# A graph network in fp32: first group in two halves, statistics aggregated ahead, one more residual buffer, second weights' loads on another queue

## The chip, the core, the metric

One core of a Trainium2 chip runs the whole program. The metric is device time per execution in microseconds (us). Engines: PE is TensorE, DVE VectorE, ACT ScalarE, POOL GpSimd, SP SyncE.

## The reference, cut

`x` is 128 graphs of 128 nodes by 256 features, `adj` one 128 x 128 matrix for all. Four layers, each with a layer norm and relu ahead and a residual around it:

```python
h = relu(layernorm(x)); x = x + gated_messages(h, adj)     # layer 0
h = relu(layernorm(x)); x = x + causal_attention(h)        # layer 1
h = relu(layernorm(x)); x = x + three_graph_convs(h, adj)  # layer 2: 256 -> 512 -> 1024 -> 256
h = relu(layernorm(x))                                     # layer 3
y = (A_hat @ h) @ W1.T + b1                                # 256 -> 512
y = relu(batchnorm(y))       # statistics over all 128 x 128 rows
y = y @ W2.T + b2            # 512 -> 256
x = x + batchnorm(y)         # again over all rows
```

The two batch norms cut the work into three parts. The first pass takes 32 groups of four graphs through everything up to `z = (A_hat h) W1` and stores z and the residual x3 to DRAM. The second pass loads z again, normalizes it and multiplies by W2. The tail normalizes once more, loads x3 where it isn't loaded yet, adds and stores.

## The kernel before

Groups 0 to 31 are generators that a fixed string interleaves. For group 0 a string FILL does so at the start, with nothing beside it but group 1 and the preparation of the weights. Products are done by a seven-product scheme (`seven`) that needs sums of quarters first. The end of the first pass and the junction:

```python
# layer 3 of a group; zp has two buffers of z, and group 31's z takes those of group 30
z = ZT[g] = [zp.tile([P, 2, T], FP, tag="z", name=f"zo_{g}_{j}") for j in range(2)]
def put(ij, pb, other):
    ...
    nc.vector.tensor_tensor(dst, pb, other, ALU.add)          # L661
    ...
    if done.count(j) == 2:
        for jj in range(2):
            nc.vector.bn_stats(stats1[:, 2 * j + jj, g, :], z[j][:, jj, :])
        if g != LAST:
            nc.sync.dma_start(Z[g][:, 2 * j : 2 * j + 2, :], z[j])   # store of z, SP
... # cut
most1 = bn_part(stats1, FC, slice(LAST), "most1")   # four bn_aggr over 31 groups
... # rest of the last group
passA.close()                                       # the first pass's memory is free
... # cut
OWN, IN_PASS, IN_Z, ROOM = 5, 7, 13, 18             # residual buffers: 18
nc.scalar.dma_start(bw2T, BW2T)                     # second weights, on ACT's queue
nc.scalar.dma_start(bw2s, BW2S)
... # cut: load_z on SP; load_x3(g, queue=nc.gpsimd), one every fourth group
for n in range(1, 1 + AT_ONCE):
    load_z(n)
last1 = bn_part(stats1, FC, slice(LAST, NG), "last1")
sc1, sh1 = bn_affine(most1, last1, FC, g1_c, be1_c, "bn1", b1_c)   # the affine
```

Of the kernel before, what the change touches and what calls it, by code (L numbers as in the profile page):

```python
# [15 lines left out]
P = 128  # L16
# [6 lines left out]
def kernel(  # L23
# [41 lines left out]
    G = 4  # L65
# [23 lines left out]
    adj_sb = const.tile([P, P], FP, name="adj_sb")  # L89
    nc.sync.dma_start(adj_sb, adj)  # L90

# [4 lines left out]
    weights = passA.enter_context(tc.tile_pool(name="weights", bufs=1))  # L96
    xin = passA.enter_context(tc.tile_pool(name="xin", bufs=4))
# [6 lines left out]
    load_x(0)  # L104
# [20 lines left out]
    stats1 = zp.tile([P, FC, NG, 6], FP, name="stats1", bufs=1)  # L125
# [108 lines left out]
    SETS = {}  # L234

    def prepare():
# [21 lines left out]
        SETS["q"], SETS["v"] = seven_of(m_qk, "m_qk"), seven_of(w_vo, "w_vo")  # L258
        yield

        nc.vector.tensor_tensor(a2T, adjT, adjT, ALU.mult)
        SETS["1"] = seven_of(w1, "w1")
        yield
        SETS["2"] = seven_of(w2, "w2")
# [40 lines left out]
    def norm(g, layer):  # L305

        xt = X[g]
        st = small.tile([P, G, 6], FP, tag="st", name=f"st{layer}_{g}")
        mv = small.tile([P, G, 2], FP, tag="mv", name=f"mv{layer}_{g}")
        for b in range(G):  # L310
            nc.vector.bn_stats(st[:, b, :], xt[:, b, :])  # L311
        for b in range(G):
            nc.vector.bn_aggr(mv[:, b, :], st[:, b, :])
        rs = small.tile([P, G], FP, tag="rs", name=f"rs{layer}_{g}")
        nc.gpsimd.tensor_scalar(rs, mv[:, :, 1], LN_EPS, None, ALU.add)  # L315
        nc.gpsimd.tensor_tensor(rs, rs, nhalf[:, :G], ALU.pow)  # L316
        sh = small.tile([P, G], FP, tag="sh", name=f"sh{layer}_{g}")
        nc.gpsimd.tensor_scalar(sh, mv[:, :, 0], -1.0, None, ALU.mult)
        nc.gpsimd.tensor_tensor(sh, sh, rs, ALU.mult)  # L319
        h = w.tile([P, G, D], FP, tag="h", name=f"h{layer}_{g}", bufs=3)  # L320
        for b in range(G):
            nc.scalar.activation(  # L322
                h[:, b, :], xt[:, b, :], AF.Relu, bias=sh[:, b : b + 1], scale=rs[:, b : b + 1]
            )
        return h

    def mixed(dst, src, aT, name, evicts):

        for c in range(src.shape[-1] // P):
            pm = bank([P, G, P], f"{name}_{c}")  # L330
            for b in range(G):
                nc.tensor.matmul(  # L332
                    pm[:, b, :], src[:, b, c * P : (c + 1) * P], aT, start=True, stop=True
                )
            evicts[c % len(evicts)](dst[:, c, :], pm.rearrange("p b n -> p (b n)"))
# [84 lines left out]
    def layer0(g):  # L420

        xt = X[g]
        h = norm(g, 0)
        yield
        gl = small.tile([P, G, 3], FP, tag="gl", name=f"gl_{g}")
        gs = w.tile([P, D], FP, tag="gs", name=f"gs_{g}", bufs=1)
        for b in range(G):
            for i in range(3):
                nc.vector.scalar_tensor_tensor(  # L429
                    gs, h[:, b, :], 1.0, gw[:, i, :], ALU.mult, ALU.mult,  # L430
                    accum_out=gl[:, b, i : i + 1],
                )
            if b == 1:
                yield
        nc.vector.tensor_tensor(gl, gl, gb[:, None, :].to_broadcast([P, G, 3]), ALU.add)
        gt = small.tile([P, G, 3], FP, tag="gt", name=f"gt_{g}")
# [4 lines left out]
        um = w.tile([P, 2, G, D], FP, tag="um", name=f"m_{g}", bufs=1)  # L441
# [4 lines left out]
        for b in range(G):  # L446
            nc.scalar.activation(bias[:, b, :], eb, AF.Copy, scale=gt[:, b, 0:1])
            nc.scalar.activation(cmb[:, b, :], ain, AF.Copy, scale=gt[:, b, 0:1])
            nc.vector.scalar_tensor_tensor(
                cmb[:, b, :], aout, gt[:, b, 1:2], cmb[:, b, :], ALU.mult, ALU.add  # L450
            )
            nc.vector.scalar_tensor_tensor(
                cmb[:, b, :], ident, gt[:, b, 2:3], cmb[:, b, :], ALU.mult, ALU.add
            )
        yield
        for b in range(G):
            nc.vector.scalar_tensor_tensor(
                bias[:, b, :], oeb, gt[:, b, 1:2], bias[:, b, :], ALU.mult, ALU.add
            )
        pc = bank([P, G, P], f"pc_{g}")  # L460
        for b in range(G):
            nc.tensor.transpose(pc[:, b, :], cmb[:, b, :], ident)
        nc.vector.tensor_copy(cmbT, pc)
        yield
        for q in range(G // 2):
# [7 lines left out]
        nc.vector.scalar_tensor_tensor(xt, bias, 0.0, xt, ALU.max, ALU.add)  # L473
        yield

    def layer1(g):

        xt = X[g]
        h = norm(g, 1)
        yield  # L480
        hT = w.tile([P, DC, T], FP, tag="dT", name=f"hT_{g}", bufs=2)
        for c in range(DC):
            pt = bank([P, G, P], f"pt_{g}_{c}")
            for b in range(G):
                nc.tensor.transpose(pt[:, b, :], h[:, b, c * P : (c + 1) * P], ident)
            evict = nc.vector.tensor_copy if c else nc.scalar.copy
            evict(hT[:, c, :], pt.rearrange("p b n -> p (b n)"))
        ex = w.tile([P, 4, 1, T // 2], FP, tag="ex", name=f"hs_{g}", bufs=2)
        hs = sums(nc.vector, quarters_t(hT), ex, ex[:, 3])
# [3 lines left out]
        qv = w.tile([P, 2, DC, 2, D], FP, tag="qv", name=f"qv_{g}", bufs=1)  # L493
# [19 lines left out]
        yield from seven(product, put, [P, 2, D], f"pqv_{g}")  # L513
# [4 lines left out]
        ps = bank([P, G, P], f"ps_{g}")  # L518
        for b in range(G):
            for c in range(DC):  # L520
                nc.tensor.matmul(  # L521
                    ps[:, b, :], qv[:, b // 2, c, 0, (b % 2) * P : (b % 2 + 1) * P],
# [3 lines left out]
        p = w.tile([P, G, P], FP, tag="p", name=f"p_{g}", bufs=1)  # L526
        nc.vector.scalar_tensor_tensor(
            p, ps, 1.0 / D**0.5, maskb[:, None, :].to_broadcast([P, G, P]), ALU.mult, ALU.add
        )
        nmax = small.tile([P, G], FP, tag="nmax", name=f"nmax_{g}")  # L530
        nc.vector.tensor_reduce(nmax, p, AX.X, ALU.max, negate=True)
        psumr = small.tile([P, G], FP, tag="psumr", name=f"psumr_{g}")
        for b in range(G):
            nc.scalar.activation(
                p[:, b, :], p[:, b, :], AF.Exp, bias=nmax[:, b : b + 1],
                accum_out=psumr[:, b : b + 1],
            )
        rsum = small.tile([P, G], FP, tag="rsum", name=f"rsum_{g}")
        nc.vector.reciprocal(rsum, psumr)
        yield  # L540
        pp = bank([P, G, P], f"pp_{g}")
        for b in range(G):
            nc.tensor.transpose(pp[:, b, :], p[:, b, :], ident)
        pT = w.tile([P, G, P], FP, tag="pT", name=f"pT_{g}", bufs=1)
        nc.vector.tensor_copy(pT, pp)
        yield
        for q in range(G // 2):
            py = bank([P, 2, D], f"py_{g}_{q}")
            for r in range(2):
                b = 2 * q + r  # L550
                nc.tensor.matmul(py[:, r, :], pT[:, b, :], v_of(b), start=True, stop=True)  # L551
            for r in range(2):
                b = 2 * q + r
                nc.vector.scalar_tensor_tensor(
                    xt[:, b, :], py[:, r, :], rsum[:, b : b + 1], xt[:, b, :], ALU.mult, ALU.add
                )
        yield
        h = norm(g, 2)
        yield
        mT = w.tile([P, DC, T], FP, tag="dT", name=f"mT_{g}", bufs=2)  # L560
        mixed(mT, h, a2T, f"pm2_{g}", (nc.vector.tensor_copy, nc.scalar.copy))
        ex = w.tile([P, 3, 1, T // 2], FP, tag="ex", name=f"ms_{g}", bufs=2)
        ms = sums(nc.vector, quarters_t(mT), ex)
        yield
        u = w.tile([P, G, H1], FP, tag="um", name=f"u_{g}", bufs=1)

        def put(ij, pb, other):
# [8 lines left out]
        yield from seven(  # L576
            rows_by_half(ms, SETS["1"], H1 // 2), put, [P, 2, H1 // 2], f"pu_{g}"
        )
        uT = w.tile([P, HC1, T], FP, tag="uT", name=f"uT_{g}", bufs=1)
        mixed(uT, u, a2T, f"pmu_{g}", (nc.vector.tensor_copy,))  # L580
        ex = w.tile([P, 3, HC1 // 2, T // 2], FP, tag="us", name=f"us_{g}", bufs=1)
        US[g] = sums(nc.vector, quarters_t(uT), ex)
# [110 lines left out]
    FILL = "paaapaaaAaBBBBBABBBBBBBppABBAApBBABBBpBBAB"  # L693
    stream = {"a": layer0(0), "p": prepare(), "B": layer1(0), "A": part(layer0, 1)}
    for k in FILL:
        next(stream[k])
    assert all(next(stream[k], k) == k for k in "aAB")
    bs, ds = part(layer1, 1), stream["p"]
    next(bs)
    for g in range(NG):  # L700
        if g + AHEAD < NG:
            load_x(g + AHEAD)
        stream = {
# [7 lines left out]
    most1 = bn_part(stats1, FC, slice(LAST), "most1")  # L711
    for _ in ds:
        pass
    passA.close()

    def bn_affine(most, last, nch, gam, bet, name, bias):
# [3 lines left out]
        share = 1.0 / NG  # L720
# [24 lines left out]
    OWN, IN_PASS, IN_Z, ROOM = 5, 7, 13, 18  # L745
# [10 lines left out]
    nc.scalar.dma_start(bw2T, BW2T)  # L756
    bw2s = second_w.tile([P, 3, FC // 2, D // 2], FP, name="bw2s_late")
    nc.scalar.dma_start(bw2s, BW2S)
# [65 lines left out]
    last1 = bn_part(stats1, FC, slice(LAST, NG), "last1")  # L824
    sc1, sh1 = bn_affine(most1, last1, FC, g1_c, be1_c, "bn1", b1_c)
# [30 lines left out]
    sc2, sh2 = bn_affine(most2, last2, DC, g2_c, be2_c, "bn2", b2_c)  # L856
# [58 lines left out]
```

## Time and profile before

The median of four runs is 2615.83 us (2615.49 to 2616.07). PE bounds the kernel; this is the page's first part, busy time, share and count of each engine:

```profile
PE 2531.7 (97%) x15215; PEld 2280.8 (87%) x15215; DVE 1918.0 (73%) x4819; ACT 1283.9 (49%) x2575; POOL 292.1 (11%) x577
```

So only the places where PE waits can give time. I follow five markers through all traces: PE's first p_x (the start is over), the product pr of groups 0, 29 and 30, PE's first po_x (second pass), PE's last po (the start of its last line in the timeline), ACT's first o (tail). Between them lie the stretches of this table. The kernel before was traced four times (the trace of the prediction and three more, told below):

| stretch | before, 4 traces | mean |
|---|---|---|
| to the first p_x | 83.61, 85.97, 83.96, 85.09 | 84.66 |
| p_x to pr of group 0 (the first turn) | 57.67 to 57.68 | 57.68 |
| pr of group 0 to 29 | 2052.9 to 2053.0 | 2052.9 |
| pr of group 29 to 30 (the turn of group 30) | 68.67 to 68.68 | 68.68 |
| pr of group 30 to first po_x (the junction) | 71.40, 71.55, 71.71, 71.39 | 71.51 |
| first po_x to last po | 203.21, 203.48, 202.79, 203.22 | 203.18 |
| last po to first o | 5.35 to 5.36 | 5.36 |
| first o to the end | 67.84, 68.43, 68.27, 68.24 | 68.20 |

From the timeline of the kernel before (start us, us, engine, line, operation; in brackets the idle time before it and what ended it; SPq and POOL DMA lines are issues, not the transfers):

```profile
2314.64 0.62 POOL L778 DMA_DIRECT2D x3i<-x  x1 [0.34 <-issue]
...
2317.39 2.13 SPq L667 DMA_DIRECT2D z<-zo  x2
...
2321.71 1.27 SPq L766 DMA_DIRECT2D zi<-z  x3
...
2323.68 0.63 DVE L661 TENSOR_TENSOR zo<-pz_z,pz_t 128x512 f32<-128x512 f32 x1
...
2326.40 1.06 POOL L778 DMA_DIRECT2D x3i<-x  x2 [11.13 <-PE pz_x L377]
```

One x3 load goes out 2.8 us ahead of the two stores of z, and none beside them until the put of pz_z at 2323.68 is over. That put (the addition that writes a part of z) has no bracket: it waits for nothing. DVE is busy with an aggregation right up to it, though (2322.79, 0.98 us), so this trace doesn't show how long before it the store of group 30's z had landed.

### The profile page before, as it was taken

To read this page: it belongs to the slowest core of one execution; us is meant where nothing else is said; L and a number is where in the kernel's file an instruction comes from. In a line of the timeline stand start us, us, engine, line, operation; in brackets the idle time before it and what ended it. 1 tells how busy PE (TensorE), PEld (TensorE's weight loads), DVE (VectorE), ACT (ScalarE), POOL (GpSimd) and SP (SyncE) were. 2 spreads that over 40 slices of the span, in tenths; PEclk is the share of its full clock that TensorE was granted. 3 is DMA by queue.
4 is the path that set the end of the run, shared out by engine and by line. 5 is a ranking of instruction groups with operands and counts; after the bars stand their busy time and mean duration, and the time that the engine had idled before them with its cause. 6 is when DMAs were issued, how large, how long until landed. Compare 5 with 4: busy or idle time off the path is not lost.

```text
span 2610.6 us, 40551 instructions
## 1 busy us (share of the span) xinstructions
PE 2531.7 (97%) x15215; PEld 2280.8 (87%) x15215; DVE 1918.0 (73%) x4819; ACT 1283.9 (49%) x2575; POOL 292.1 (11%) x577
## 2 busy tenths in 40 slices
PE   4999999999999999999999999999999999989995
PEld 3999999999999999999999999999999999978875
DVE  7877777777777777777777777777777776567776
ACT  3544544444445454454444444554445444336656
POOL 1111111111111110111111111111011111010001
PEclk7999999999999999999999999999999999999998
DMA  3000000000000000000000000000000000034559
GB/s 132 15 33 33 33 23 27 33 33 33 26 26 31 33 33 33 33 33 17 33 33 33 33 25 25 33 33 33 33 33 29 21 25 25 25 143 163 176 174 398
DMA packets 49544, 143.06 MB, mean 55 GB/s; under 512 B 4146, under 2 KB 23108, under 8 KB 45380
## 3 DMA queue, kind: packets, MB, share of 16 engines
q1 hardware_dynamic: 40708, 111.37, 11.8%
q0 software_dynamic: 7632, 27.79, 2.9%
q8 instruction: 120, 1.97, 0.3%
q10 hardware_dynamic: 1008, 1.31, 0.1%
q14 instruction: 76, 0.62, 0.1%
HBM read 73.48 MB, written 66.98 MB: 54 GB/s over the span
## 4 chain that ended last, share of the span: by engine, by line
PE 91%; DMA 3%; DVE 2%; ACT 2%; issue 1%; POOL 0%; ACTq 0%; DVEq 0%; POOLq 0%; SPq 0%
PE p_x L377 17%; PE p_x L360 9%; PE p_z L377 8%; PE pmu L332 4%; PE p_z L360 4%; PE pu_x L360 4%; PE p_y L377 4%; PE pz_x L377 4%; PE pm L332 2%; PE pg L332 2%; PE ps L521 2%; PE py L551 2%; PE pqv_x L501 2%; PE p_y L360 2%; PE pm L469 2%; PE pqv_x L496 2%
## 5 line engine op out<-in xcount | busy, mean ns | idle before, releaser
L322 ACT ACTIVATE h<-x,sh,rs 128x256 f32<-128x256 f32 x512 | 268.8, 589 | 367.0 <-POOL sh L319 367.0
L377 PE MATMUL p_x<-uT,w 128*128 128x256 f32 x1024 | 242.2, 379 | 0.0
L608 ACT ACTIVATE h2T<-h2T 128x512 f32<-128x512 f32 x192 | 120.5, 628 | 227.3 <-DVE h2T L607 227.3
L377 PEld LDWEIGHTS p_x<-uT,w 128*128 128x128 f32 x1024 | 189.7, 190 | 23.1
L311 DVE BATCH_NORM_STATS2 st<-x 128x6 f32<-128x256 f32 x512 | 190.8, 415 | 4.9 <-DMA x<-in_x_dram 2.8
L315 POOL TENSOR_SCALAR rs<-mv 128x4 f32<-128x4 f32 x128 | 29.9, 233 | 1403.8 <-ACT h2T L608 1053.0
L429 DVE SCALAR_TENSOR_TENSOR gs<-h,gw 128x256 f32<-128x256 f32 x384 | 161.0, 419 | 28.4 <-ACT h L322 23.0
L392 ACT COPY p_t<-p_x 128x512 f32<-128x512 f32 (+1 forms) x192 | 96.6, 503 | 108.2 <-PE p_x L377 101.4
L316 POOL TENSOR_TENSOR rs<-rs,nhalf 128x4 f32<-128x4 f32 x128 | 148.9, 1163 | 0.0
L332 PEld LDWEIGHTS pmu<-a2T,u 128*128 128x128 f32 x1024 | 119.5, 192 | 15.1 <-issue 14.8
L360 PEld LDWEIGHTS p_x<-w,h2T 128*128 128x128 f32 x1024 | 124.3, 192 | 3.3
L574 ACT ACTIVATE u<-u 128x512 f32<-128x512 f32 x96 | 60.5, 631 | 134.8 <-DVE u L573 134.8
L789 ACT ACTIVATE zi<-zi,sh_bn,sc_bn 128x512 f32<-128x512 f32 x124 | 97.4, 812 | 55.9 <-DMA zi<-z 30.0
L360 PE MATMUL p_x<-w,h2T 128*128 128x128 f32 x1024 | 124.6, 275 | 0.0
L377 PE MATMUL p_x<-us,w_s 128*128 128x256 f32 x512 | 121.2, 379 | 0.0
L377 PE MATMUL p_x<-uT,w_s 128*128 128x256 f32 x512 | 121.1, 379 | 0.0
L377 PE MATMUL p_y<-uT,w 128*128 128x256 f32 x512 | 121.1, 379 | 0.0
L377 PE MATMUL p_z<-us,w 128*128 128x256 f32 x512 | 121.0, 379 | 0.0
L377 PE MATMUL p_z<-us,w_s 128*128 128x256 f32 x512 | 120.9, 379 | 0.0
L332 PE MATMUL pmu<-a2T,u 128*128 128x128 f32 x1024 | 119.8, 275 | 0.0
L637 DVE TENSOR_TENSOR x<-pr,x 128x512 f32<-128x512 f32 x64 | 43.7, 683 | 90.4 <-PE pr L636 90.4
L377 PEld LDWEIGHTS p_z<-us,w 128*128 128x128 f32 x512 | 97.3, 190 | 13.2
(289 smaller groups left out, 6174.7 us busy)
## 6 DMA issues: line engine op xcount, KB each, us to landing
z<-zo SPq DMA_DIRECT2D x62, 512.0 KB, 2.6
zi<-z SPq DMA_DIRECT2D x31, 1024.0 KB, 4.9
x<-in_x_dram SPq DMA_DIRECT2D x32, 512.0 KB, 4.0
x<-x POOLq DMA_DIRECT2D x32, 512.0 KB, 3.4
out_dram<-x3i SPq DMA_DIRECT2D x30, 512.0 KB, 13.5
x3i<-x POOLq DMA_DIRECT2D x21, 512.0 KB, 9.4
x3i<-x SPq DMA_DIRECT2D x11, 512.0 KB, 4.7
w<-in_L_gnn_W_dram SPq DMA_DIRECT2D x1, 2048.0 KB
```

Source lines behind the costliest of these rows:

```text
L311: nc.vector.bn_stats(st[:, b, :], xt[:, b, :])
L316: nc.gpsimd.tensor_tensor(rs, rs, nhalf[:, :G], ALU.pow)
L322: nc.scalar.activation(h[:, b, :], xt[:, b, :], AF.Relu, bias=sh[:, b : b + 1], scale=rs[:, b : b + 1])
L332: nc.tensor.matmul(pm[:, b, :], src[:, b, c * P : (c + 1) * P], aT, start=True, stop=True)
L360: nc.tensor.matmul(pb[:, rr, :], a_r[r][:, c, rr * P : (rr + 1) * P], b_r[r][:, c, :wide], start=(first and rr == 0 and c == 0), stop=(c = ...
L377: nc.tensor.matmul(pb[:, jj, :], b_r[r][:, c, at : at + P], a_r[r][:, c, :], start=(first and jj == 0 and c == 0), stop=(c == nk - 1), ski ...
L392: nc.scalar.copy(t, pb)
L429: nc.vector.scalar_tensor_tensor(gs, h[:, b, :], 1.0, gw[:, i, :], ALU.mult, ALU.mult, accum_out=gl[:, b, i : i + 1],)
L469: nc.tensor.matmul(pm[:, r, :], cmbT[:, b, :], h[:, b, :], start=True, stop=True)
L574: nc.scalar.activation(dst, dst, AF.Relu)
L608: nc.scalar.activation(dst, dst, AF.Relu)
L789: nc.scalar.activation(z, z, AF.Relu, bias=sh1[:, j : j + 1], scale=sc1[:, j : j + 1],)
```

## The change

Four parts, which I call H, A, R and W. **H**: group 0 goes through layers 0 and 1 and the first half of layer 2 as two halves of two graphs, so that one half's norm can run beside the other's products; the halves use plain products, as the sums of the seven-product scheme need the whole group. FILL is written anew for it, and a part of the preparation of the weights moves behind the halves. **A**: the four aggregations over 31 groups become four over 30, emitted a group earlier; two groups are left for the end. **R**: adj and stats1 move into the first pass's memory, and a 19th residual buffer fits. **W**: the second weights are loaded from SP's queue, not ACT's.

```diff
-    load_x(0)
+    X[0] = xin.tile([P, G, D], FP, tag="x", name="x_0")
+    for i in range(2):
+        half = slice(i * G // 2, (i + 1) * G // 2)
+        nc.sync.dma_start(X[0][:, half, :], x[half].rearrange("b n d -> n b d"))
... (norm, layer0, layer1 take a list of graphs bs; in layer1, for a half:)
-        yield from seven(
-            rows_by_half(ms, SETS["1"], H1 // 2), put, [P, 2, H1 // 2], f"pu_{g}"
-        )
+            for b in bs:
+                pb = bank([P, H1], f"pu_{g}_{b}")
+                for c in range(DC):
+                    nc.tensor.matmul(pb, mT[:, c, b * P : (b + 1) * P], w1[:, c, :], ...)
... (A)
+        if g == LAST:
+            most1 = bn_part(stats1, FC, slice(LAST - 1), "most1")
-    most1 = bn_part(stats1, FC, slice(LAST), "most1")
     for _ in ds:
         pass
+    last1 = bn_part(stats1, FC, slice(LAST - 1, NG), "last1")
     passA.close()
... (R; adj_sb moves likewise)
-    stats1 = zp.tile([P, FC, NG, 6], FP, name="stats1", bufs=1)
+    stats1 = weights.tile([P, FC, NG, 6], FP, name="stats1")
-    OWN, IN_PASS, IN_Z, ROOM = 5, 7, 13, 18
+    OWN, IN_PASS, IN_Z, ROOM = 6, 8, 14, 19
... (W)
-    nc.scalar.dma_start(bw2T, BW2T)
+    nc.sync.dma_start(bw2T, BW2T)
-    nc.scalar.dma_start(bw2s, BW2S)
+    nc.sync.dma_start(bw2s, BW2S)
```

## The prediction

> **What bounds the kernel now.** I read the 40 slices of the page first, then the table of windows over both ends, then the chain of work that ended last and the timeline of each engine there.
>
> ```profile
> PE   4999999999999999999999999999999999989995
> PEclk7999999999999999999999999999999999999998
> DMA  3000000000000000000000000000000000034559
> ```
>
> PE is full in 36 of 40 slices; in the waits of PE between 200 and 2250 us nothing is listed. Time can be had only in the first slice, around slices 36 and 37, and in the last three. The windows (busy us of PE, PEld, DVE, ACT, POOL, then granted clock, DMA share, GB/s) give the ends:
>
> ```profile
> 20.00:40.00 20.00, 7.21 (x21) 4.33 (x21) 15.63 (x49) 7.72 (x18) 5.92 (x9) 0.63 0.42 138
> 40.00:60.00 20.00, 15.26 (x70) 12.10 (x70) 15.06 (x38) 9.64 (x23) 0.00 (x0) 0.77 0.00 1
> 60.00:80.00 20.00, 14.79 (x78) 13.32 (x79) 14.88 (x41) 7.91 (x17) 2.81 (x4) 0.83 0.12 46
> 80.00:100.00 20.00, 20.00 (x121) 18.30 (x120) 17.89 (x60) 11.88 (x24) 3.31 (x8) 1.00 0.00 1
> ...
> 2320.00:2360.00 40.00, 30.67 (x127) 25.03 (x126) 30.86 (x67) 20.89 (x39) 4.23 (x7) 0.87 0.66 244
> ...
> 2580.00:2600.00 20.00, 8.04 (x54) 6.71 (x52) 9.22 (x15) 8.06 (x12) 0.58 (x2) 0.80 1.03 418
> ```
>
> Up to 80 us PE idles about 35 us and runs at a reduced clock; from 80 us it is full. At 2320 to 2360 it loses 9.3 us. In the tail the DMA engines are full at 418 GB/s. Pieces of the chain in the start (start us, us, what):
>
> ```profile
> 25.90 3.40 PE pm L469 x8
> ...
> 36.72 0.61 ACT h L322
> 37.37 1.96 PE pt L485 x7
> ...
> 52.22 0.50 ACT p L534 x2
> ...
> 64.56 0.61 ACT h L322
> 65.22 3.98 PE pm L332 x16
> ...
> 83.77 0.43 PE p_x L377 x2
> ```
>
> One group walks through two layers with nothing beside it: every norm is a walk DVE, POOL, ACT, PE. My marker for "the start is over" is the first p_x at L377, at 83.6 us in the timeline. The junction between the passes, from the timeline:
>
> ```profile
> 2324.82 0.99 DVE L675 BATCH_NORM_AGGREGATE mv_most<-stats 128x2 f32<-128x186 f32 x1
> 2324.96 1.13 PE L377 MATMUL pz_x<-gT,bw1T_s 128*128 128x256 f32 x4 [1.10 <-DVE zo L661]
> ...
> 2328.89 0.98 DVE L675 BATCH_NORM_AGGREGATE mv_most<-stats 128x2 f32<-128x186 f32 x1
> ...
> 2334.24 2.08 PE L800 MATMUL po_x<-zo,bw2T 128*128 128x256 f32 x4 [8.15 <-ACT zo L789]
> ```
>
> Four aggregations over 31 groups stand among the last statistics, and PE's second pass waits 8.15 us for what hangs on them.
>
> **What the Trainium skill says.** "TensorE: Matmul & The Clock Gate", Part 1 on the HAM clock gate: the array runs at half rate after about 3.4 us of idleness and needs about 3.4 us of work to come back. The trace agrees: pm x16 took 3.98 us at 65.22 and 1.79 us in the steady state. So pulling work closer saves twice, and an idle gap that only shrinks from 8 to 6 us still costs the slow phase. "SBUF — State Buffer", Who interferes with whom: a tensor_tensor with both inputs in SBUF contends with GpSimd's reads, under an exclusive lock. The trace agrees: the norm's four POOL steps took 0.24 + 0.23 + 1.04 + 0.28 = 1.8 us from 9.09 on, but 0.31 + 1.06 + 1.45 + 0.22 = 3.0 us from 33.52 on, when DVE did 128x1024 subtractions. "ScalarE: Activation LUTs", What ACT_TABLE_LOAD costs, has about 1283 ns; the trace shows 1.28 us for each. "DMA: Bandwidth & Descriptors", Where 436 GB/s comes from, puts the fabric at 435; the tail's 418 is near it, so there only bytes count.
>
> **The start, step by step.** I walked the new order of instructions on each engine with the durations above; all times here are my estimates from them. The first x comes in halves, but POOL does both halves' scalings before the first power, so h starts at about 11 us as before (11.29). The second weights (w1) are wanted on DVE at about 14 us, perhaps before they land; the gates of half one are ready at about 18 us, where the sigmoid's table load holds them, against 20.3. Its transposed mixing matrix is copied at about 22.5 to 23 (before 25.15), x is done at 27.5 (before 31.4), h of layer 1 at 33.6 (before 36.7), the first copies of hT at 35.3 (before 39.4). Half two comes some 4 us behind: its norm waits for DVE behind the copy of hT, its h ends at 39.9, its hT at 42.7.
>
> The plain product costs PE more. qv per group is 16 matmuls of 256 columns worth 0.43 us each (8 of them in pairs of 128 columns), 6.9 us for 7 x 0.86 = 6.0; u is 8 of 512 columns at 0.86, 6.9 for 6.0. That is 0.9 us each. It takes away the sums (8 x 0.42 us on DVE) and three rounds of kept copies and additions from the chain.
>
> Scores of half two stand before those of half one on PE. They come at about 47.5 (before, the whole group's at 50.5), exp at 49.2 to 50.3 (before 52.2 to 53.9). Then ACT takes sigmoid's table for group 1 and exp's table again, 2 x 1.28 us, before the exp of half one, which ends at about 54.8: here most of the lead is lost. From there: py at 56 to 57.2, x at 58.2, statistics at 59.5, POOL 1.7 us, h at about 61.7, where the kernel before had 65.2. PE's work from there to the marker at full clock: mixing and transposes 0.9, u 6.9, group 1's pm 1.7, pmu 3.6, transposes of bw1 and bw2 with small ones 2.1, sum 15.2; the slow clock adds some 2.2 (as 3.98 against 1.79) and the gap for copying mT 0.6. The marker is then at 61.7 + 18.0 = 79.7, **3.9 us earlier**.
>
> Some DVE work now lies behind the marker: eight subtractions for bw2t and bw1T at 0.34 us, ahT and vecs, 3.2 us together, in a window where DVE was busy 17.89 of 20. By my walk the hT copy that PE needs comes about 7.7 us after the marker and PE wants it at 9.5, so it is mostly hidden; I charge **0.5 us**.
>
> **The junction.** The 30 groups are aggregated in the last-but-one turn, where DVE has 19 to 26 us of work in 40; its pT copy and PE's py keep 1 us of slack there, the later norm about 3. So 4 x 0.98 us moves to where it is free. At the end, put of pz_z starts at 2323.05 rather than 2323.68, the last product at 2324.6 rather than 2324.96, its copy on ACT ends at 2326.35, the two last statistics at 2327.6, two aggregations at 2327.85; before, the affine's first step was at 2330.14. **2.3 us earlier**, as everything behind it (3.1 us of small steps, then ACT, then PE) is unchanged. The weights bw2T and bw2s were issued by ACT at 2326.14, after its last copy; now SP issues them behind the last stores of z, at about 2320. They carry 0.9 MB, 2.1 us at 418 GB/s, so the zi loads behind them on SP are later; the first zi is wanted at 2336.2 - 2.3 = 2333.9 and should be there by 2333.
>
> **The tail.** A 19th buffer takes one 0.52 MB load of x3 out of the full stretch (13 late loads for 14), into the second pass whose DMA share is 0.49: 0.52 MB / 418 GB/s = **1.25 us**. The room comes from adj and stats1 (3.5 KB per partition), which now go with the first pass.
>
> Sum: -3.9 + 0.5 - 2.3 - 1.25 = -6.95 us; 2616.0 - 7.0 = **2609.0 us**.
>
> **Rivals.** (a) The halves do not help: two walks on in-order queues hold each other up (POOL's powers, ACT's h behind h, the second exp table), and the marker stays near 83. For it: DVE was busy 15 of 20 us in each window, so it is nearly as much the bound as latency. Against it: the chain shows each engine waiting in turn. Time about 2613. (b) The halves overlap better than my walk: DVE's 57.5 us of work up to 80 with almost no idling after a first x at 6 us would put the marker near 70 to 72. For it: PE waits 8.1 and 6.2 us for h alone. Time about 2601. (c) At the junction the zi or bw2T load takes the place of the aggregation, since DMA runs at 410 to 426 GB/s from 2323 to 2337 and one more x3 load joins; the 2.3 us shrinks to 1 or less. Time about 2610.5. (d) The tail is hidden anyway, because ACT's 64 activations (45.3 us) pace it; against it, the DMA engines stay full for 20 us after ACT ends.
>
> **Range.** The start is the wide term: 0 to 10 us; junction 1 to 2.5; tail 1 to 1.5; backlog up to 2. Together 2603 to 2613.5. Two per cent is 52 us, more than all idle time that the change touches, so within 2% is nearly certain.
>
> **What would show it.** Right: first p_x near 79.7; full PE windows from there; L675's 31-group aggregations gone from the end and the affine's first step 2.3 us after less waiting; between last pz_x and first po_x some 6 us; 13 loads of x3 in the tail, its full stretch 1.25 us shorter. Wrong: PE idle in 80 to 130 us waiting for DVE; po_x waiting for a DMA; stalls of PE in the last-but-one turn; or the marker beyond 75 to 83.

## The result, and the profile after

The changed kernel takes 2612.15 us (median of four runs, 2611.57 to 2613.66) against 2615.83: a ratio of 0.9987, with a 95% interval from 0.997 to 1.0004, "same" at 2%. The number lies in the predicted range, 3.15 us above the point.

That says little about the reasons. The 40 slices of the page after:

```profile
PE   5999999999999999999999999999999999989996
PEclk8999999999999999999999999999999999989998
```

The first slice is a step fuller; the dip at slice 36 is as in the kernel before. The same windows as in the prediction (busy us of PE, PEld, DVE, ACT, POOL; clock, DMA share, GB/s):

```profile
20.00:40.00 20.00, 9.52 (x33) 6.44 (x33) 16.63 (x48) 4.04 (x12) 5.33 (x8) 0.66 0.39 130
40.00:60.00 20.00, 13.16 (x70) 10.05 (x69) 15.18 (x56) 13.20 (x29) 3.44 (x9) 0.90 0.00 1
60.00:80.00 20.00, 17.33 (x73) 12.07 (x72) 11.63 (x35) 5.58 (x14) 3.49 (x8) 0.76 0.00 0
80.00:100.00 20.00, 19.99 (x117) 17.77 (x117) 18.18 (x60) 13.79 (x29) 1.96 (x4) 1.00 0.12 47
2320.00:2360.00 40.00, 29.21 (x121) 23.33 (x119) 26.00 (x60) 20.24 (x37) 4.21 (x7) 0.83 0.71 254
```

In the start PE is busier (17.33 for 14.79 between 60 and 80 us, in part because its clock is lower there, 0.76 for 0.83), and from 80 us it is full. But between 2320 and 2360 PE lost 1.5 us instead of gaining two (29.21 for 30.67), although DVE has less to do there (26.00 for 30.86). The start, in PE's timeline:

```profile
63.77 1.22 PE L352 MATMUL pm<-a2T,h 128*128 128x128 f32 x4 [2.67 <-ACT h L338]
...
66.48 5.11 PE L635 MATMUL pu<-w,mT 128*128 128x512 f32 x8
...
73.16 3.60 PE L635 MATMUL pu<-w,mT 128*128 128x512 f32 x8
...
82.27 1.99 PE L397 MATMUL p_x<-uT,w 128*128 128x256 f32 x8
```

The last half's h reaches PE at 63.77, where the whole group's did at 65.22, and the marker is at 82.27. The two pu lines are the same work: 5.11 us where the half clock ends on the way (at 69.52 by the trace's clock records), 3.60 at the full clock. Now the junction:

```profile
2317.22 2.12 SPq L731 DMA_DIRECT2D z<-zo  x2
...
2317.93 1.18 POOL L848 DMA_DIRECT2D x3i<-x  x2 [3.79 <-issue]
...
2319.44 0.38 SPq L826 DMA_DIRECT2D bw2T<-BW2T  x1
...
2326.82 0.69 DVE L725 TENSOR_TENSOR zo<-pz_z,pz_t 128x512 f32<-128x512 f32 x1 [4.06 <-DMA z<-zo]
...
2328.16 2.08 PE L397 MATMUL pz_x<-gT,bw1T_s 128*128 128x256 f32 x4 [4.46 <-DVE zo L725]
...
2328.17 1.27 SPq L836 DMA_DIRECT2D zi<-z  x3
...
2336.55 2.08 PE L870 MATMUL po_x<-zo,bw2T 128*128 128x256 f32 x4 [6.31 <-ACT zo L859]
```

The last line looks like success: the wait of po_x is down from 8.15 to 6.31 us. But po_x is late, because the product before it is: pz_x waits 4.46 us for the put of pz_z, and that put waits 4.06 us for the store of group 30's z, whose buffer it overwrites. The two stores were issued at 2317.2 and 2319.0, the two x3 loads between them, the second weights behind them. By queue, what moved between 2320 and 2323 us (q0 is POOL's queue, q1 SP's; packets, MB, share of 16 engines):

```profile
q0 software_dynamic: 195, 0.74, 96.1%
q1 hardware_dynamic: 3, 0.01, 0.7%
```

The first store had moved by then (0.52 MB on q1 from 2317.2 to 2320), so it is the second that the put waits for, and it all but stood still while the x3 loads moved. The chain of waits can't be read here: the page after gives PE 5% of it, and the reason is in its pieces.

```profile
2318.56 0.55 POOL x3i L848
2319.11 14.62 issue
2333.77 1.04 POOL sc_bn L189
```

It follows POOL's queue back, whose 14.62 us of "issue" are a wait for DVE's affine, and so leaves out the store. The timeline of the engine that was late shows it.

One more loss is far from all this, in the stretch from pr of group 29 to that of group 30, which grew from 68.68 to 69.42 us:

```profile
2231.38 1.78 DVE L739 BATCH_NORM_AGGREGATE mv_most<-stats 128x2 f32<-128x180 f32 x2
...
2234.90 1.78 DVE L739 BATCH_NORM_AGGREGATE mv_most<-stats 128x2 f32<-128x180 f32 x2
...
2249.39 1.13 PE L380 MATMUL pu_x<-w,mT 128*128 128x256 f32 x4 [0.55 <-DVE mT L355]
```

The scheduler put the early aggregations ahead of x and its norm; what follows from that is told with the sixth experiment. By stretches, the one trace after against the mean of four before: start 82.27 - 84.66 = -2.39; p_x to pr of group 0 +0.35; turn of group 30 +0.74; junction 73.87 - 71.51 = +2.36; second pass 201.77 - 203.18 = -1.41; tail 66.88 - 68.20 = -1.32. The sum is -1.7, in the interval of the ratio (0.0013 x 2615.8 = 3.4 us faster, from 7.8 faster to 1.0 slower).

### The profile page after: what moved, and what is told of

Its sections match the earlier page's. It is cut to its first block, busy times and chain, and to the rows that moved or that the text cites. A ratio compares the mean times of both kernels' runs of the same rounds, so it can differ in the third digit from the quotient of the medians. Undisturbed runs are those within 1.5% of the kernel's fastest.

```text
span 2610.6 us, 40551 instructions
## 1 busy us (share of the span) xinstructions
PE 2534.5 (97%) x15209; PEld 2278.0 (87%) x15209; DVE 1914.1 (73%) x4820; ACT 1283.5 (49%) x2575; POOL 296.9 (11%) x589
## 5 line engine op out<-in xcount | busy, mean ns | idle before, releaser
L331 POOL TENSOR_SCALAR rs<-mv 128x4 f32<-128x4 f32 (+1 forms) x131 | 31.5, 240 | 1396.3 <-ACT h2T L672 1026.8
L332 POOL TENSOR_TENSOR rs<-rs,nhalf 128x4 f32<-128x4 f32 (+1 forms) x131 | 149.8, 1144 | 0.0
```

Source lines behind the costliest of these rows:

```text
L332: nc.gpsimd.tensor_tensor(rs, rs, nhalf[:, :n], ALU.pow)
```

## The experiments

Twelve runs, of which ten were timed in five rounds. The theory after the first traces: H gains some 3 us, the moved aggregation costs 0.74 in its new place, and at the junction a store stretched by x3 loads takes more than the moved aggregation gives. The main rival: the kernels are alike but for luck in the clock and the transfers.

### 1. The kernel before against itself

No edit.

> The kernel before, unchanged, to learn which of its runs its trace shows: its profiled run took 2612.5 us, the four other runs 2615.5 to 2616.1. Theory: the profiled run was a lucky one and 2615.8 is the kernel's usual time, so the median is 2615 to 2616.5 and, if this profile falls on a usual run, the extra 3 us stand in one place, either before the first p_x (83.6 us in the first trace) or between the last pz_x and the first po_x (2334.2 us). Rival: the profile itself makes a run 3 us faster: then this profiled run is again at 2612 to 2613 with the timed ones at 2616.

Measured 2615.28 us, ratio 0.9996 (0.9982 to 1.001). So a ratio of 0.9996 is nothing, and one of 0.9987 is barely something. Its profiled run took 2615.95 us, so it isn't the profile that makes a run faster. Its trace has the first p_x at 85.97 us, 2.4 us after the trace that the prediction was made from; experiments 10 and 11 return to that.

### 2. The halves alone

The changed kernel with A, R and W undone (aggregation of 31 groups at the end, 18 buffers, weights on ACT, adj and stats1 where they were).

> Only the first part of the change: the first group in two halves with plain products. Theory (the traces): the first p_x comes at 82.3 us against 83.6, the 31-group aggregations are back at the end, so the time is 1.3 us under that of before, about 2614.5. Rival A (my prediction): 3.9 us less, 2612. Rival B: the start alone carries the whole measured gain because the usual run of before starts later than its trace: 2612 too, but then with a first p_x still at 82.3 and a first p_x of a usual run of before near 86.

Measured 2613.05 us, ratio 0.999 (0.9977 to 1.0002). First p_x at 81.92. The turn of group 30 takes 68.70 us, as in the kernel before, so H isn't what stretches it. The junction takes 73.23 us, which nobody expected of this kernel: po_x waits 9.7 us for bw2T, though with A undone its affine is no earlier than before. The zi loads went out at 2324.05, 1.2 us ahead of bw2T, where in the kernel before they went out 4.4 us ahead of it. That suggests, without showing it, that in the kernel before those weights come only just in time.

### 3. The weights back on ACT's queue

```diff
-    nc.sync.dma_start(bw2T, BW2T)
+    nc.scalar.dma_start(bw2T, BW2T)
-    nc.sync.dma_start(bw2s, BW2S)
+    nc.scalar.dma_start(bw2s, BW2S)
```

> The changed kernel, but the two loads of the second weights back on the queue of ACT. Theory: these 0.9 MB, issued at 2319.4 beside the last two stores of z, hold the stores back by 0.9 MB / 418 GB/s = 2.2 us, and DVE's put of pz_z waits for them 4.1 us; without them the put comes some 2.2 us earlier, the first po_x at about 2334.3 instead of 2336.55, the time 2610. Rival: the two x3 loads on POOL's queue (2317.9) are what the stores share with: the wait stays at 4 us, the time at 2612. Second rival: po_x waits for bw2T instead: time 2612 or more with a DMA as the releaser of po_x or of its weight load.

Measured 2614.52 us, ratio 0.9994 (0.9982 to 1.0007). The put still waits 2.8 us for the store, with 0.9 MB less beside it than the 4.06 us of the changed kernel, and po_x waits 8.7 us for bw2T: junction 74.32, as in the second rival. So, beside the x3 loads, the second weights account for a part of the put's wait, the smaller one.

### 4. The x3 loads on SP's queue

```diff
         if n % 4 == 3 and n // 4 < IN_PASS:
-            load_x3(n // 4)
+            load_x3(n // 4, nc.sync)
```

There they stand behind the zi loads, so behind the last put.

> The changed kernel, but the eight loads of x3 in the second pass are issued by SP, in turn behind the loads of zi, so none of them runs beside the last stores of z. Theory: the two early x3 loads are 1.05 MB, 2.5 us at 418 GB/s; the put of pz_z comes 2.5 us earlier (wait 4.1 down to 1.6), the first po_x at about 2334, the time 2609.7. Rival: only the weights' loads matter (the stores and they are on one queue): wait unchanged, time 2612. If zi loads come later through x3 loads standing between them on SP, PE waits for ACT on zi in the second pass and the gain is given back.

Measured 2607.51 us, ratio 0.9969 (0.9956 to 0.9981). All its five runs are below all runs of both kernels (the changed one's lowest is 2611.57), though its interval and that of the changed kernel just overlap. The put of pz_z starts at 2323.40 after 0.25 us of waiting for PE, and the junction takes 69.22 us: 2.29 less than before, the -2.3 of the prediction. All that the junction had lost was one wait and the half clock after it. The wait fell by 3.8 us, not by the 2.5 us that 1.05 MB take at 418 GB/s: the store had not only shared the engines with the x3 loads, it had stood behind them (the two queue lines above).

### 5. x3 on SP, weights on ACT

Experiment 4 with the edit of experiment 3.

> The fourth experiment (x3 loads on SP) with the loads of bw2T and bw2s on ACT's queue again, as in the kernel before. Theory: they are issued at about 2326, behind the zi and x3 loads that SP has by then, and with the affine 2.3 us earlier PE's first po_x waits for bw2T, as it did in the second and third experiments: po_x at about 2334, junction some 71 us, time 1.5 to 2 us above the fourth, near 2609.3. Rival: with x3 behind them they land in time, no wait for bw2T shows, and the time is 2607.5: then moving those loads was not needed.

Measured 2610.81 us, ratio 0.9982 (0.997 to 0.9995), 3.4 us above experiment 4. The list of waits of PE between 2320 and 2340 us (waiting, what for: us in all, times, longest):

```profile
PE po_x L870 <- DMA bw2T<-BW2T: 8.7, 1, 8.7
```

The junction takes 71.66 us for 69.22. So in this order W is needed: it is what lets the earlier affine reach PE. The 1.5 to 2 us expected were too few: in the traces it is 2.4 for the junction and 1.8 for a longer tail (68.84 us for 67.00), less a start 1.5 us earlier.

### 6. The aggregation after x

Experiment 4, with a read of the last group's x ahead of the aggregations, so that the scheduler can't put them before it:

```diff
+        if after is not None:
+            nc.vector.tensor_copy(mv[:, :, 0], after[:, 0, :nch])
...
-            most1 = bn_part(stats1, FC, slice(LAST - 1), "most1")
+            most1 = bn_part(stats1, FC, slice(LAST - 1), "most1", after=X[LAST])
```

> The changed kernel with its x3 loads on SP (the fourth experiment, 2607.51 us), and the aggregations of 30 groups made to read the x of the last group once (a copy of one column into their output), so that they cannot stand before that group's x is finished. Theory: the two pairs of aggregations at 2231.4 and 2234.9 us delayed x, the norm and mT of the turn of group 30 by 0.74 us; after x DVE idles 4.8 us waiting for ACT's h2T, and there they cost nothing. The turn between the pr of group 29 and that of group 30 comes back from 69.42 to about 68.7 us, and the time is 0.7 us lower, near 2606.8. Rival: the last turn is longer for another reason (more buffers and other addresses), and it stays 69.4. Second rival: the aggregations now delay h2s and mT by up to 3 us, and the turn is 70 to 72 us.

Measured 2606.78 us, ratio 0.9966 (0.9953 to 0.998): the fastest median of all, 0.73 us under experiment 4, though the intervals of the two overlap. The trace is sharper: the turn takes 68.70 us, not 69.42. From its timeline:

```profile
2241.17 2.61 DVE L741 BATCH_NORM_AGGREGATE mv_most<-stats 128x2 f32<-128x180 f32 x3
...
2245.06 0.69 DVE L363 TENSOR_TENSOR h2s<-h2T 128x512 f32<-128x512 f32 x1 [1.28 <-ACT h2T L664]
...
2248.68 1.12 PE L380 MATMUL pu_x<-w,mT 128*128 128x256 f32 x4
```

Three of the four aggregations now fill time in which DVE waits for ACT's h2T (4.83 us of it in the changed kernel), and pu_x, which waited 0.55 us for mT there, waits for nothing. In the changed kernel the 3.6 us of aggregations stood before x and its norm. The first pair cost nothing: the next copy on DVE (pT) starts at 2233.10 in both traces. The second pair, 1.78 us, went into a place where DVE waits only 0.71 us for PE's py in experiment 6, and x came at 2236.59 for 2235.69. PE got h2s and mT later through ACT's h and h2T, and 0.72 us of that weren't covered.

### 7. and 8. One buffer less; aggregation at the end

Experiment 7 is experiment 4 with 18 buffers; experiment 8 is experiment 7 with A undone.

```diff
-    OWN, IN_PASS, IN_Z, ROOM = 6, 8, 14, 19
+    OWN, IN_PASS, IN_Z, ROOM = 5, 7, 13, 18
... (8 only; adj and stats1 are put back too)
-            most1 = bn_part(stats1, FC, slice(LAST - 1), "most1")
+    most1 = bn_part(stats1, FC, slice(LAST), "most1")     # after the last turn
```

> The fourth experiment (x3 loads on SP) with 18 residual buffers in place of 19: one 0.52 MB load more in the tail. Theory: the tail from ACT's first o to the end is 68.2 us as in the kernels with 18 buffers, not 67.0, and the time is 0.9 to 1.25 us above that of the fourth experiment, 2608.4 to 2608.8. Rival (the tail is hidden anyway, by ACT): the same time, 2607.5. The junction stays as in the fourth experiment, some 69 us from pr of group 30 to the first po_x.

> The seventh kernel (x3 loads on SP, 18 buffers, second weights on SP) with the aggregation put back where it was: of 31 groups, at the end. Against the seventh this is the clean worth of aggregating ahead. Theory: the junction is 2.3 us longer (about 71.4 us from pr of group 30 to first po_x), the turn of group 30 is 0.74 us shorter (68.68), so 1.5 us slower than the seventh: near 2610. Rival: in this order too something else, the put that waits for the store or the weights bw2T, sets the junction, and the two kernels differ by less than 0.5 us.

Experiment 7: 2607.82 us, ratio 0.9973 (0.996 to 0.9985). The tail takes 68.11 us and not 67.00; by the ratios it is 0.0004 x 2615 = 1.0 us slower than experiment 4, too little to be told apart by the times alone, and below the 2608.4 expected. The five other traces with 19 buffers have tails of 66.88, 67.95, 67.01, 66.36 and 67.30 us, and a sixth, in experiment 5, 68.84; the seven with 18 lie between 67.84 and 68.43. The means are 67.3 and 68.2, so a buffer is worth 0.9 us. With the second weights on SP in all of them, it is 1.2: five traces with 19 have a mean of 66.9, two with 18 of 68.1. Why the two kernels that have 19 buffers and the weights on ACT show 67.95 and 68.84 I didn't follow up.

Experiment 8: 2611.55 us, ratio 0.9985 (0.9973 to 0.9998), 3.1 us above experiment 7 by the ratios. In the traces the junction takes 71.58 us for 69.20 and the turn of group 30 68.72 for 69.41: net 1.7 us for A, near the 1.5 expected. The rest is a start later by 1.1 us in the trace, which is within the spread of one kernel, and a second pass longer by 1.1, which is the clock: half clock until 6.0 us after the first po_x, for 3.9 in experiment 7.

### 9. x3 on POOL, first into the buffers of z

The theory of the store has a rival that experiment 4 leaves alive: that the queue matters, or the place behind zi, and not the bytes beside the store.

```diff
-            pool, tag = (x3p, "x3") if k < OWN else (zp, "z") if k < IN_PASS else (late, "x3l")
+            pool, tag = (zp, "z") if k < 2 else (x3p, "x3") if k < IN_PASS else (late, "x3l")
```

> The changed kernel, x3 loads on POOL as in it, but the first two x3 loads are given the buffers of z that the last group still reads, so that POOL's queue can start none before the second pass has read them; the six buffers of their own come after. Nothing stands beside the stores of z at 2317 to 2327 then. Theory (the x3 loads at 2317.93 stretch the store that the put of pz_z waits for): the put waits for no store, the junction from pr of group 30 to the first po_x falls from 73.87 to about 69.2 us although the loads stay on POOL, and the time is near that of the fourth experiment (2607.5), perhaps 0.5 us more as loads come later. Rival (it is the queue, POOL's, or the place behind zi on SP that mattered): the put still waits about 4 us and the junction stays near 73.9, time 2612. Second rival: with x3 late another wait appears in the tail, and the time is over 2609 with a short junction.

Measured 2611.48 us, ratio 0.999 (0.9976 to 1.0004), and the experiment missed its purpose. The scheduler put the loads of the third and fourth x3, whose buffers were free, ahead of the first two:

```profile
2317.75 1.18 POOL L848 DMA_DIRECT2D x3i<-x  x2 [3.79 <-issue]
```

The put waited 3.38 us for the store as ever (junction 72.85). It tells nothing of the queue, only that other buffers don't help.

### 10. and 11. Two more looks at the kernel before

No edit.

> The kernel before, unchanged, for one more start: its first p_x was at 83.61 us in the trace that the prediction was made from and at 85.97 in the second. Theory: the start varies by some 2 us between runs of one kernel, because PE's clock windows run freely, and 83.61 was an early one; this run is at 83.5 to 86.5, more likely above 85. Rival: 85.97 was the odd one, and this run is at 83.6.

> As the run before it, for the spread of the start: first p_x between 83.5 and 86.5 us.

Single runs, 2613.21 and 2614.37 us; first p_x at 83.96 and 85.09: both in the range expected, the first below the 85 that was thought more likely. The four starts of the kernel before are 83.61 to 85.97 us, mean 84.66. The ten traces with halves have 82.27, 81.92, 81.35, 82.70, 82.33, 81.25, 82.38, 81.24, 82.12 and 80.56, mean 81.81. No trace of one kind reaches into the other, and the halves, together with the preparation that moves behind them (no run parts the two), are worth 2.85 us at this marker. Much of the spread is the clock: in the trace at 85.97 PE ran at half clock from 56 to 73 us, in that at 83.61 it had 3 us of full clock from 59.5 on and was back at full from 69.7. In the clock records of all traces, every stretch at half clock in the start lasts a multiple of 3.41 us (3.41 to 23.89), and in the four traces of the kernel before the first of them begins at 20.4 to 22.3 us.

### 12. x3 on POOL, held behind the affine

```diff
             R[g] = pool.tile([P, G, D], FP, tag=tag, name=f"x3i_{g}")
+            if k < OWN and g < ROOM:
+                nc.gpsimd.tensor_copy(R[g][:, 0, 0:1], sh1[:, 0:1])
```

> The ninth experiment failed in its edit: the scheduler put the loads of the third and fourth x3 first, so two loads stood beside the stores of z at 2317.75 us all the same. Here each of the six x3 loads of the second pass that have buffers of their own is held by a one-column copy on POOL of the affine's shift into its buffer; the order of instructions shows all six behind the affine's step on POOL (2331 us). The loads stay on POOL's queue; stores, second weights and zi are those of the changed kernel. Theory (the bytes of two x3 loads beside the store of z stretch it, and the put of pz_z waits for it): no wait of the put over 0.5 us, the junction from pr of group 30 to the first po_x falls from 73.87 to 69.2 us, and the time is about 2607.5 to 2608.5. Rival (the stores wait for the second weights' loads on their own queue, SP, or POOL's queue as such matters): the put still waits 3 to 4 us, the junction stays at 73 to 74, the time near 2611.5.

Measured 2607.12 us, ratio 0.9967 (0.9953 to 0.9981). From its timeline:

```profile
2321.28 0.69 DVE L725 TENSOR_TENSOR zo<-pz_z,pz_t 128x512 f32<-128x512 f32 x1 [0.20 <-DMA z<-zo]
...
2330.10 3.28 POOL L850 DMA_DIRECT2D x3i<-x  x6
2330.15 2.08 PE L872 MATMUL po_x<-zo,bw2T 128*128 128x256 f32 x4 [6.27 <-ACT zo L861]
```

Same queue, same bytes in all, only 12.4 us after the second weights and not beside the store: the put's wait is 0.20 us, and the junction takes 69.21. The rival of the queue falls. Stores and second weights are those of the changed kernel, so the two x3 loads are what held the store up. The Trainium skill would have told me to look: "DMA: Bandwidth & Descriptors", Issuing engines are not separate DMA queues, says that transfers issued from different engines run on the same 16 DMA engines and interleave. The queues share the engines, but the interleaving isn't even (0.01 MB beside 0.74 above). The second store was issued at 2319.0 in the changed kernel and the put was released at 2326.82, 7.8 us later; here it was issued at 2317.3 and the put ran at 2321.28, 4.0 us later.

## Why the prediction was right or wrong

Right in class and range, for reasons that were half right: the start and the tail gave less than said, the junction lost where it should have won, and a piece of luck made up for a part. By its own steps:

**The start, -3.9.** The direction is right and rival (a) falls: -2.85 us over fourteen traces. The mis-sized term is "h at about 61.7": it came at 63.77. The exp of half one ended at 55.8 (predicted 54.8), its py took 2.08 us at half clock (predicted 1.2), and norm and h gave the rest. PE's walk from there, predicted as 18.0, took 18.50. Part of the gain that is left is hidden in the number 83.6: the prediction's marker before was the earliest of four. Two small readings in it are off: the PE line has 37 nines, not 36, and 3.98 us is a span where 1.79 is a time from start to start (the steady span is 1.95), so the slow clock's 2.2 is 2.0.

**The backlog, +0.5.** Measured +0.35 (58.02 for 57.67), as a slightly longer first turn: hidden for the most part, as said.

**The junction, -2.3.** The sum was right: with the store out of the way it is 71.51 - 69.21 = 2.30. The step that failed is its setting, "put of pz_z starts at 2323.05". It took for granted that the put waits only for PE; in the trace before, an aggregation filled the time up to it and hid the question. It looked for trouble only later, in rival (c), at bw2T and zi. The trouble was the second store of group 30's z. Its buffer is reused, two x3 loads had come to stand ahead of it, and the second weights, which the change put behind the stores on SP for good reason, behind it. The junction was 2.36 us longer instead, a miss of 4.7, shown by experiments 4 and 12. Why two loads of x3 are ready at 2317.93 in the changed kernel, where the second one waited for pz_x in the kernel before, stays open. It comes from A or R, as experiment 2 (H alone) has the loads as before and experiment 3 (without W) as after; that it is R, since these buffers lie over memory of the first pass and R changed what lies where, is only argued.

**"4 x 0.98 us moves to where it is free."** It wasn't free: 0.72 us, shown by experiment 6. DVE has idle time in that turn, but the scheduler took the aggregations at the earliest place and not at the idle one. The slack ahead of x was about as said (1 us; 0.71 measured), but two aggregations, 1.78 us, were put into it. The prediction named the sign ("stalls of PE in the last-but-one turn"), and the sign was there.

**The weights' loads** were predicted to be in time on SP, and were. That on ACT's queue they would have held up PE (experiments 3 and 5) the prediction hadn't said.

**The tail, -1.25.** Measured 0.9 (67.3 for 68.2, seven traces each), 1.1 in the pair that differs in this alone, 1.2 with the second weights on SP throughout. Rival (d) falls.

**Luck.** After a junction 2.4 us longer, the second pass was 1.41 us shorter. In the changed kernel the half clock ended 2.8 us after the first po_x, in the kernel before 5.0 to 6.1 us after it; PE loses half of that time, so this gives some 1.4 us. In the ten traces with halves the half clock ends 2.8 to 6.0 us after it, so another trace of the changed kernel need not show the gain. The prediction had no term for it.

With both faults mended (experiment 6) the change gives 2606.78 us, less than the 2609.0 predicted.

## What to carry to other kernels

When work is moved ahead of a wait, ask of every instruction that will now run earlier what else it needs: a buffer that a store still reads makes the store's landing a part of the path, and a transfer issued beside it can make it later, from another queue too. Which one does is a matter for a run: here 1.0 MB on POOL's queue held the store up, 0.9 MB behind it on its own queue alone did not. "There is idle time in that stretch" isn't yet "it is free": look where the scheduler will put it, and tie it with a dependency if it must stand later. And trace the kernel before several times before taking a microsecond from one trace: its start alone varied by 2.4 us.

## What the Trainium skill lacked or had wrong

- "TensorE: Matmul & The Clock Gate", Part 1: it puts the change to the full clock at around 4 us of sustained work, 500 ns more or less, since the windows run freely. These runs agree on the spread, not on the length. After the same 8.1 us gap, the half clock lasted for 5.3, 6.1, 5.0 and 5.7 us of renewed work in four runs of the kernel before, so the gap cost PE half of that, 2.5 to 3.0 us, on top of itself; the "about 3.4 us" that the prediction took from the page was too short each time.
- "DMA: Bandwidth & Descriptors": right about the shared engines, but without a number for what loads on another queue do to a store's landing. Here a 512 KB store on SP's queue with 0.9 MB of loads behind it released the put 4.0 us after its issue; with two 512 KB loads issued from POOL just ahead of it, 7.8 us, and for 3 us of these SP's queue moved 0.01 MB.
- No page gives the time of BATCH_NORM_AGGREGATE: 0.97 us alone over 180 elements per partition (1.78 us for two in a row), 0.33 for two over 12.
